# The Dice gate of a recommender kernel's attention sums: from one ScalarE and one VectorE operation to two VectorE operations

## The chip, the cores and the metric

The kernel runs on one core of one Trainium2 chip. Its time is the device time of that core in microseconds (us). In what follows PE is TensorE, DVE is VectorE, ACT is ScalarE, POOL is GpSimd and SP is SyncE, as the profile calls them.

## The reference

For 16384 users, each with 69 item ids (`batch_user`) and one label id, rows of 96 floats are taken from an embedding table of 100001 rows. An attention network gives each of the 69 rows one weight, the weighted rows are summed in 10 windows of fields, and a small network follows.

```python
def _dice(x, alpha, eps):
    p = jax.nn.sigmoid(_bn_eval(x, eps))
    return (alpha * (1.0 - p) + p) * x

u = emb[batch_user]
ql = emb[batch_label[:, 0]]
q = jnp.broadcast_to(ql[:, None, :], u.shape)
z = jnp.concatenate([q, u, q - u, q * u], axis=-1)
h = _dice(z @ W1 + b1, a1, EPS_DICE)
h = h @ W2 + b2
att = h @ W3 + b3
eff = (batch_user < ITEM_NUM)[..., None]
pre = jnp.where(eff, u * att, 0.0)
pooled = jnp.einsum('gf,bfe->bge', window, pre).reshape(u.shape[0], G * E)
x = jnp.concatenate([pooled, ql], axis=-1)
h = _dice(_bn_eval(x @ Wf1 + bf1, EPS_BN), af1, EPS_DICE)
h = _dice(_bn_eval(h @ Wf2 + bf2, EPS_BN), af2, EPS_DICE)
return h @ Wf3 + bf3
```

The change concerns the first `_dice`, on the sums `z @ W1 + b1` of 64 hidden units. With p the sigmoid of the sum x, and a the unit's alpha, it is (a + (1 - a) p) x.

## The kernel before

**Tiling.** The users are cut into 32 blocks of 512. A block has 69 chunks of 512 (user, field) places: 64 main chunks of 8 users with 64 fields each, and 5 tail chunks of one field for all 512 users. Two chunks make a pair, and the whole kernel is a sequence of 1104 pairs. All data is fp32.

**Steps.** Python unrolls everything. A dictionary `plan` holds, for each step (one pair is fetched in each), a list of work that is put out in that order on all engines; the tile framework adds the semaphores and keeps the order as written (`manual_schedule`). Each engine runs its own instructions in order. In step i, in this order, stand:

- every fourth step, `attend_rows` of the pairs i-6 to i-3: PE multiplies four y tiles by the folded second and third layer (`prow`, L414), and ACT copies the result (`row`, L416);
- `attend_tail` of pair i-3, for tail chunks alone (`pa`, L423, and DVE's `pre`, L424);
- every fourth step, `spread`: PE transposes `row` (`patt`, L431) and DVE turns it into weights for the pooling (`rw`, L436);
- `hidden` of pair i-2: PE's sums `ph` (L396 to L403), then the Dice gate that makes `y` (L405 to L407);
- ACT's own row fetches for this step (`scalar_rows`, L301, 16 rows of 384 bytes each, with the offsets loaded into registers at L286);
- `pool` of pair i-7: 16 matmuls of `rw` with the rows (`acc`) and DVE's copy into `pooled` (L470);
- `fetch` of pair i: the gathers of 128 rows each by POOL into `u` (L266), PE's transposes of them (`ptr`; the helper `read_rows` at L325 records these and the matmuls of `acc`), and for each of the two chunks DVE's copy `uT` (L376) and product `quT` (L379, or L386 in a tail chunk).

Between these, spread over the steps, stand the label rows of the next block (`q`, gathered by POOL as well, 128 gathers in all) and the final network of a finished block (`p`, L502 to L522, with gates of its own at L483 to L485, which the change leaves alone).

**Fetches.** A pair needs 8 gathers of 128 rows. Of the 8832 of all pairs, 8587 are indirect DMAs issued by POOL; the other 245 are done row by row with plain DMAs into `ring`, by SP (13952 rows) and ACT (17408 rows). A transpose or `acc` matmul that reads `ring` waits for its rows by a semaphore.

**Buffers that matter here.** `u` has 14 buffers of one pair each, and a pair is read for the last time by `pool`, 7 steps after its fetch. `ptr` has 2 PSUM buffers, `ph` has 2, `acc` has 1; `y` has 6 buffers in SBUF. `a1c` and `na1c` are columns of 128 scalars in SBUF that hold a and 1 - a.

**The gate before.** ACT makes the sigmoid from `ph` (PSUM) into `y` (SBUF), then in a second operation y becomes a + (1 - a) y in place, and DVE multiplies by `ph`.

Of the kernel before, what the change touches and what calls it, by code (L numbers as in the profile page):

```python
# [14 lines left out]
AF = mybir.ActivationFunctionType  # L15
ALU = mybir.AluOpType
# [46 lines left out]
def chunk_of(c):  # L63

    n, k = divmod(c, NCH)
    if n == NBLK - 1 and k >= EARLY:
        k = NMAIN + k - EARLY if k < EARLY + NTAIL else k - NTAIL
    return n, k
# [47 lines left out]
def rec_kernel(  # L116
# [12 lines left out]
    nc = tc.nc  # L129
# [68 lines left out]
    a1c = NEAR.of(wn, "a1")  # L198
    na1c = const.tile([P, 1], F32, name="na1c")
# [189 lines left out]
    def hidden(i, uT, quT):  # L389

        ph = ps_h.tile([P, 512], F32, tag="h", name=f"ph{i}")
        places = [chunk_of(2 * i + j) for j in range(2)]
        sums = [ph[j * H1 : (j + 1) * H1, :] for j in range(2)]
        for (n, k), p in zip(places, sums):
            if k >= NMAIN:
                nc.tensor.matmul(p, Cq, qTs[n % 2], start=True, stop=False)  # L396
        for j, ((n, k), p) in enumerate(zip(places, sums)):
            if k < NMAIN:
                nc.tensor.matmul(p, As[n % 2][:, k // 4, :], uT[j], start=True, stop=False)  # L399
            else:  # L400
                nc.tensor.matmul(p, A, uT[j][0:E], start=False, stop=False)  # L401
        for j, p in enumerate(sums):
            nc.tensor.matmul(p, Wp, quT[:, j, :], start=False, stop=True)  # L403
        y = ypool.tile([P, 512], F32, tag="y", name=f"y{i}")
        nc.scalar.activation(y, ph, AF.Sigmoid, scale=S_DICE)  # L405
        nc.scalar.activation(y, y, AF.Identity, bias=a1c, scale=na1c)  # L406
        nc.vector.tensor_mul(y, ph, y)  # L407
        return y

    def attend_rows(b, n):  # L410
# [156 lines left out]
    def hidden_of(k):  # L567
        return lambda: ys.__setitem__(k, hidden(k, *hs[k]))
# [186 lines left out]
```

## Time and profile before

| What | Value |
|---|---|
| Median of 3 runs | 13779.89 us (13749.68 to 13785.55) |
| The profiled execution's own time | 10926.71 us |
| Its span, first to last instruction | 10924.9 us |
| Granted TensorE clock in it, mean | 0.745 |
| PE busy | 8862.0 us (81%) |
| POOL busy | 8226.3 us (75%) |
| DVE busy | 4285.5 us (39%) |
| ACT busy | 1897.5 us (17%) |
| DMA engines, mean | 42 GB/s |

The profile is one execution. Its own time is 1.8 us above its span, and 2853 us below the median of the runs: the runs were longer than the profiled execution by a factor of 1.261. A duration read from the profile is therefore a part of 10926.71 us.

A line of the groups reads: line of the code, engine, operation, output<-input by the tiles' names, shapes, number; then total busy time in us and mean of one in ns; then the idle time of that engine just before these instructions, and what ended most of it. "issue" means that the engine waited for nothing that the profile shows. A line of the timeline reads: start in us, length in us, engine, line, operation, tiles, number, and in brackets the idle time before it.

### The profile page before, as it was taken

The page shows a single profiled execution, that of the slowest core. Times are in us where ns is not written, and L with a number is a line of the kernel's source. Part 1 is how long each engine was busy: PE and PEld are TensorE (multiplying, and loading weights), DVE is VectorE, ACT ScalarE, POOL GpSimd, SP SyncE. Part 2 cuts the span into 40 slices and gives each one's busy share as a digit, 9 for nine tenths or more (in the row PEclk, how much of TensorE's full clock was granted, in tenths as well). Part 3 has the DMA queues.
Part 4 walks back from the last instruction along what each step waited for, and adds up shares of the span by engine and source line. Part 5 has one row for each costly group of instructions (what it writes and reads, how often), then busy time and mean ns, then how long its engine had stood idle before and what let it go on. Part 6 is the DMA issues. An engine that isn't in the chain of part 4 may idle for free.

```text
span 10924.9 us, 172203 instructions
## 1 busy us (share of the span) xinstructions
PE 8862.0 (81%) x41797; PEld 4319.5 (40%) x41797; DVE 4285.5 (39%) x7535; ACT 1897.5 (17%) x2761; POOL 8226.3 (75%) x8721
## 2 busy tenths in 40 slices
PE   7878878788887888888878778878888887888878
PEld 3333434343333344333433333334343333433335
DVE  4334333333333333433333333333333333333334
ACT  1111111111111111111111111111111111111112
POOL 7777777777777777777777777777777777777776
PEclk7767777777777777767777777777777777777777
DMA  2212211121111212212111121112212112122111
GB/s 49 42 42 44 42 42 41 42 44 42 42 42 42 44 41 42 42 41 44 42 42 41 42 44 42 42 42 42 44 42 42 42 41 44 42 42 41 42 41 36
DMA packets 344467, 458.51 MB, mean 42 GB/s; under 512 B 202354, under 2 KB 202866, under 8 KB 343330
## 3 DMA queue, kind: packets, MB, share of 16 engines
q0 software_dynamic: 278880, 428.92, 18.7%
q1 hardware_dynamic: 29762, 11.82, 0.5%
q10 hardware_dynamic: 34816, 6.75, 0.4%
q8 instruction: 336, 5.51, 0.2%
q14 instruction: 673, 5.51, 0.2%
HBM read 446.74 MB, written 0.07 MB: 41 GB/s over the span
## 4 chain that ended last, share of the span: by engine, by line
POOL 49%; issue 21%; PE 17%; DMA 12%; DVE 0%; ACT 0%; ACTq 0%; POOLq 0%; DVEq 0%
POOL u L266 48%; DMA u<-in_rows,ids 12%; PE p L502 4%; PE acc L325 4%; PE ph L399 3%; PE ph L403 2%; PE ptr L325 2%; POOL q L266 1%; PE prow L414 1%; PE pa L423 1%; PE ph L396 0%; PE ph L401 0%; PE pc L348 0%; PE patt L431 0%; ACTq L301 0%
## 5 line engine op out<-in xcount | busy, mean ns | idle before, releaser
L266 POOL DMA_INDIRECT u<-in_rows,ids x8587 | 8104.3, 944 | 2620.1 <-issue 2428.2
L325 PE MATMUL ptr<-ident,u 128*96 128x128 f32 x8587 | 2002.8, 332 | 1940.1 <-DMA u<-in_rows,ids 1892.9
L407 DVE TENSOR_TENSOR y<-ph,y 128x512 f32<-128x512 f32 x1104 | 763.5, 692 | 4377.1 <-ACT y L406 4119.6
L325 PEld LDWEIGHTS ptr<-ident,u 128*96 128x96 f32 x8587 | 1139.7, 149 | 2701.4 <-DMA u<-in_rows,ids 2262.6
L325 PEld LDWEIGHTS acc<-rw,u 128*96 128x96 f32 x15930 | 1677.0, 187 | 1204.3 <-issue 977.6
L376 DVE COPY uT<-ptr 96x512 f32<-96x512 f32 x2208 | 1494.1, 677 | 1488.6 <-PE ptr L325 1485.2
L325 PE MATMUL acc<-rw,u 128*96 128x20 f32 x15930 | 1792.5, 258 | 57.8 <-DVE rw L436 41.7
L405 ACT ACTIVATE y<-ph 128x512 f32<-128x512 f32 x1104 | 658.6, 597 | 6308.6 <-PE ph L403 5822.7
L399 PE MATMUL ph<-uT,A 128*64 128x512 f32 x4096 | 1649.8, 883 | 0.0
L403 PE MATMUL ph<-quT,wn 96*64 96x512 f32 x4416 | 1585.2, 788 | 0.0
L379 DVE TENSOR_TENSOR quT<-ptr,qT 96x512 f32<-96x512 f32 x2048 | 1380.2, 674 | 0.0
L406 ACT ACTIVATE y<-y,wn,na1c 128x512 f32<-128x512 f32 x1104 | 898.1, 813 | 36.6
L403 PEld LDWEIGHTS ph<-quT,wn 96*64 96x64 f32 x4416 | 440.7, 188 | 1041.5 <-issue 1040.8
L502 PE MATMUL p<-pooled,wf 96*100 96x512 f32 (+1 forms) x1400 | 693.1, 644 | 0.0
L399 PEld LDWEIGHTS ph<-uT,A 128*64 128x64 f32 x4096 | 264.1, 175 | 616.2 <-issue 608.8
L416 ACT COPY row<-prow 128x512 f32<-128x512 f32 (+1 forms) x277 | 161.6, 583 | 1791.9 <-PE prow L414 1179.1
L470 DVE COPY pooled<-acc 96x160 f32<-96x160 f32 x1008 | 419.9, 417 | 117.6 <-PE acc L325 116.9
L414 PE MATMUL prow<-y,v 128*32 128x512 f32 x2208 | 453.6, 891 | 1.4 <-DVE y L407 1.1
L502 PE MATMUL p<-pre,V 96*100 96x512 f32 (+1 forms) x700 | 394.9, 710 | 3.0 <-DVE x L485 2.7
L502 PEld LDWEIGHTS p<-pooled,wf 96*100 96x100 f32 x1400 | 259.5, 198 | 332.6 <-issue 332.6
L436 DVE SCALAR_TENSOR_TENSOR rw<-patt,bb,wn 128x320 f32<-128x320 f32 x554 | 276.2, 539 | 143.6 <-PE patt L431 142.9
L431 PE MATMUL patt<-ident,row 128*128 128x128 f32 x1108 | 224.9, 340 | 25.1 <-DVE pre L424 22.7
(72 smaller groups left out, 2445.8 us busy)
## 6 DMA issues: line engine op xcount, KB each, us to landing
ring<-in_rows ACTq DMA_DIRECT2D x17408, 0.4 KB
ring<-in_rows SPq DMA_DIRECT2D x13952, 0.4 KB
u<-in_rows,ids POOLq DMA_INDIRECT x8587
ids<-in_idx SPq DMA_DIRECT2D x8, 560.0 KB, 3.9
q<-in_emb,ids POOLq DMA_INDIRECT x128
wf<-in_far SPq DMA_DIRECT2D x1, 1209.0 KB, 6.4
wn<-in_near SPq DMA_DIRECT2D x1, 236.0 KB, 2.8
ids<-in_idx SPq DMA_DIRECT2D x1, 140.0 KB, 2.3
```

The source lines that it names most:

```text
L266: nc.gpsimd.indirect_dma_start(out=dst, out_offset=None, in_=table, in_offset=bass.IndirectOffsetOnAxis(ap=index, axis=0),)
L325: ins = op(out, ring[:, at[0]].bitcast(F32) if at else u[:, 4 * (c % 2) + t, :], other, **how)
L376: nc.vector.tensor_copy(uT[j][0:E], ptr)
L379: nc.vector.tensor_tensor(quT[:, j, :].rearrange("e (s f) -> e s f", f=FM), ptr.rearrange("e (s f) -> e s f", f=FM), by_field(q[:, k * NS ...
L399: nc.tensor.matmul(p, As[n % 2][:, k // 4, :], uT[j], start=True, stop=False)
L403: nc.tensor.matmul(p, Wp, quT[:, j, :], start=False, stop=True)
L405: nc.scalar.activation(y, ph, AF.Sigmoid, scale=S_DICE)
L406: nc.scalar.activation(y, y, AF.Identity, bias=a1c, scale=na1c)
L407: nc.vector.tensor_mul(y, ph, y)
L414: nc.tensor.matmul(pr[32 * k : 32 * (k + 1), :], v2, ys[b + k], start=True, stop=True)
L470: nc.vector.tensor_copy(pooled[n][:, :, k * NS : (k + 2) * NS].rearrange("e g s -> e s g"), pa.rearrange("e j s g -> e (j s) g"),)
L502: nc.tensor.matmul(p1, w[:, h * DH : (h + 1) * DH], x, start=(k == 0), stop=(k == KTOP - 1))
```

## The change

ACT makes the sigmoid s of the sums alone. DVE then makes the gate in two operations, each with one operand in PSUM and one in SBUF: first y = (s (1 - a)) x, then y = (x a) + y, with x in `ph`. The second reads what the first wrote.

```diff
         y = ypool.tile([P, 512], F32, tag="y", name=f"y{i}")
         nc.scalar.activation(y, ph, AF.Sigmoid, scale=S_DICE)
-        nc.scalar.activation(y, y, AF.Identity, bias=a1c, scale=na1c)
-        nc.vector.tensor_mul(y, ph, y)
+        nc.vector.scalar_tensor_tensor(y, y, na1c, ph, ALU.mult, ALU.mult)
+        nc.vector.scalar_tensor_tensor(y, ph, a1c, y, ALU.mult, ALU.add)
         return y
```

Nothing else differs. The line numbers stay the same: L406 was ACT's second operation and is DVE's first one, L407 was DVE's multiplication and is DVE's second operation.

## The prediction

> **What bounds the kernel now.** I first read the page's engine rows, then the groups, because busy shares alone would point at TensorE (81%) and not at POOL (75%). The groups and the waits say otherwise. From the page:
>
> ```profile
> span 10924.9 us, 172203 instructions
> PE 8862.0 (81%) x41797; PEld 4319.5 (40%) x41797; DVE 4285.5 (39%) x7535; ACT 1897.5 (17%) x2761; POOL 8226.3 (75%) x8721
> ...
> L266 POOL DMA_INDIRECT u<-in_rows,ids x8587 | 8104.3, 944 | 2620.1 <-issue 2428.2
> L325 PE MATMUL ptr<-ident,u 128*96 128x128 f32 x8587 | 2002.8, 332 | 1940.1 <-DMA u<-in_rows,ids 1892.9
> L407 DVE TENSOR_TENSOR y<-ph,y 128x512 f32<-128x512 f32 x1104 | 763.5, 692 | 4377.1 <-ACT y L406 4119.6
> ...
> L405 ACT ACTIVATE y<-ph 128x512 f32<-128x512 f32 x1104 | 658.6, 597 | 6308.6 <-PE ph L403 5822.7
> ...
> L406 ACT ACTIVATE y<-y,wn,na1c 128x512 f32<-128x512 f32 x1104 | 898.1, 813 | 36.6
> ```
>
> POOL's idle time is "issue": it waits for nobody. With the 128 gathers of q there are 8715 gathers, each 0.944 us long and followed by 0.305 us of issue (2660.8 us of idle over 8715). 8715 x 1.249 = 10885 us of a span of 10924.9. In the timeline the last gather ends at 10887.7, so 37 us follow it, and the first starts at 3.3. POOL's wait list shows no single wait above 0.3 us apart from one of 2.0 at the start. TensorE waits 1893 us in 2264 pieces for what POOL fetches, DVE 4120 us for L406, ACT 5823 us for TensorE. TensorE's 81% is no sign of a bound: its granted clock averages 0.745[...]. The gathers' rhythm is the bound; everything else runs beside it.
>
> [...] The two new operations have one SBUF tensor, one PSUM tensor and a pointer scalar in SBUF[...]. L424 already has that kind of operands (pa in PSUM, bb a pointer, uT in SBUF), so I looked at gathers beside it in the timeline:
>
> ```profile
> 1048.57 0.94 POOL L266 DMA_INDIRECT u<-in_rows,ids  x1 [0.30 <-issue]
> ...
> 1049.82 0.94 POOL L266 DMA_INDIRECT u<-in_rows,ids  x1 [0.30 <-issue]
> ...
> 1050.10 1.40 DVE L424 SCALAR_TENSOR_TENSOR pre<-pa,bb,uT 96x512 f32<-96x512 f32 x2
> ...
> 1051.07 0.94 POOL L266 DMA_INDIRECT u<-in_rows,ids  x1 [0.30 <-issue]
> ...
> 1052.32 0.95 POOL L266 DMA_INDIRECT u<-in_rows,ids  x1 [0.31 <-issue]
> ```
>
> Two such operations lie over two gathers, and the starts stay 1.25 us apart. Over all records of the trace the mean distance from one gather's start to the next is 1249.1 ns where an L424 lies over it, 1248.7 where none does. [...] the trace has 0.692 us for L407. [...] I price the dependent pair at two full durations and a gap.
>
> **The change part by part.** *Removed:* 1104 ACT operations of 0.813 us = 898 us (L406 of before), and 1104 DVE multiplications of 0.692 = 764 us. *Added:* 2208 SCALAR_TENSOR_TENSOR on DVE, 128x512. The nearest rows are L424 (0.739 median, 96x512) and L485 (0.751, 100x512); lower bound the 0.692 of L407, upper 0.80 for a pointer read that costs more. I take 0.745: 2208 x 0.745 = 1645, so DVE gains 881 us (764 to 1003), from 4286 to 5167 us or 47% of the span. That is hidden: on POOL nothing depends on it directly. The built order shows the rows of PE, POOL and SP unchanged, ACT 1104 fewer, DVE 1104 more.
>
> *The chain of one y.* Before (timeline at 5007): sigmoid from 5006.99 to 5007.59, L406 from 5007.62 to 5008.43, DVE from 5008.46 to 5009.15: 1.56 us from the sigmoid's end. After: a hop of 0.04, 0.745, a gap of 0 to 0.2 for the second operation's wait on the first (I take 0.05), 0.745: 1.58 us (1.42 to 1.84). So y, and the PSUM bank ph, come at about the same time. Behind the waiting second operation DVE queues pooled (L470), uT (L376) and quT (L379), for which TensorE's transposes wait through two ptr banks. In 1032 of 1104 cases DVE stood idle for L406, 4.0 us on average, so it starts earlier and ends no later. In the other 72 it was behind, and pays up to 881/1104 = 0.80 us: 57 us in all, on DVE. What covers that is the 1893 us that TensorE waits for gathers, and behind it u's 14 buffers, of which a pair is released 7 pairs later: POOL would be held only when TensorE falls several pairs (of 9.9 us each) behind. Cost 0. If that cover went, the next thing late would be the transposes and then POOL's waits for u.
>
> *ACT's row fetches* (L301, 16 a pair, and the offset loads L286) stand behind L406 in ACT's queue. In the timeline they start at 5007.68, just after L406 was issued at 5007.62, so they move forward by about 0.63 us a pair. No matmul on ring waits in the trace (idle 0.0 before them), and SP's queue is not touched: gain 0, unless ACT is the bound (below).
>
> *Head and tail.* Before the first gather nothing changes. In the 37 us behind the last one, the chain runs through matmuls, the row copy and g (L483, L484), and has no L406 after 10887; allow 0.3 us either way.
>
> **Sum:** 10926.7 us (the profiled execution's own time, 1.8 around its span) + 0, give or take 1 us. The runs' median is 13779.89, 1.261 times that. The profile does not show why. [...] I take the change as 0 of the median too: **13780 us**. A measurement of this kernel can tell about 0.3% (41 us) from no change; its three runs span 0.26%.
>
> **Rivals.** *Slower: DVE and gathers exclude each other in the timed runs.* Suppose the unseen 2853 us are gathers held up by DVE: 2853 / 4286 = 0.67 us for each busy us. Then 881 more cost 587: 14367 us, 4.3% slower. It decides from 0.047 us for each added us of DVE (41 / 881). The one fact for it is the unexplained gap; against it, gathers are not longer beside any DVE operation in the trace (0.5 ns). Chance 0.10. *TensorE is the bound in the timed runs.* Were its clock 0.5 throughout, its busy time would be 8862 x 0.745 / 0.5 = 13204, close to the median. The chain of y is then still as long, so mostly no change; if the 72 late cases all count, 57 us more: 13837. Chance 0.09, of which 0.04 for over 0.3%. *Faster: ACT's queue is the bound in the timed runs.* In the trace ten row fetches take 2.95 us, so 17408 take 5135; with 544 offset loads at 2.17 and 1898 busy this is 8216 us or 75%. ACT would have to stretch 1.68 times for 13780 while the whole stretches 1.26. It would gain 1104 x 0.63 = 696: 13084. Chance 0.09. *The change does not do what it says:* excluded, the rows were counted above.
>
> **How the numbers follow.** Gathers remain the bound and nothing moves: 0.64, with TensorE's unchanged part 0.05 gives 0.69 within 0.3%. Slower: 0.10 + 0.04 + 0.04 for a small unseen cost = 0.18. Faster: 0.09 + 0.04 for a small version of ACT's relief = 0.13. The range leaves out the two large rivals (0.19) and takes in the small ones, which I let reach 1% either way: 13640 to 13920.
>
> **What would show it.** Right: L266 again 8587 times at 944 with idle only for issue; DVE near 5170 us, ACT near 1000; the new lines near 0.745; DVE's wait for ACT now for L405 and about 0.8 us shorter each. Wrong: gathers longer or further apart than 1.25 us, POOL waiting for PE's acc, or a span that changes by more than 33 us (0.3% of 10926.7). If the span stays and the timed median moves, the fault is in carrying the profiled execution over to the timed runs.

## The result, and the profile after

The changed kernel took 13663.19 us (median of 5 runs, 13658.30 to 13688.42), the kernel before 13762.13 us beside it: a ratio of 0.9932, 95% interval 0.9915 to 0.9949. That is a gain of 0.7%, where no change was forecast.

The program's runs come in two lengths: about 10.93 ms and about 13.6 to 13.8 ms. The profiled execution of before that the prediction rests on was of the **short kind**; the runs that were to be predicted, and the profile after, are of the **long kind**. In both, a gather (in the changed kernel 0.944 us in the short kind and 0.945 in the long one), the sigmoid (0.597 in both) and the two gate operations (0.747 and 0.751 against 0.745 and 0.751) themselves take the same time. What differs is the time between them: POOL's idle time before the gathers is 2620 us in the one and 5285 in the other.

The page of the changed kernel, long kind. The line that begins with "PE 28%" is the chain that ended last: the work and the waits met when one goes back from the last instruction, each time to what released it, as shares of the span. ACTq in it is ACT's sequencer, which issues ACT's row fetches and holds them in one queue with ACT's operations (in the prediction's trace each of the 1088 groups of 16 fetches stands whole between two ACT operations, and the earliest operation behind one starts 0.04 us after its end):

```profile
span 13660.8 us, 171082 instructions
PE 9255.3 (68%) x41797; PEld 4797.0 (35%) x41797; DVE 5106.9 (37%) x8639; ACT 992.1 (7%) x1657; POOL 8237.3 (60%) x8721
...
PE 28%; issue 25%; ACTq 21%; another core or an unknown queue 14%; DVE 10%; ACT 2%; POOL 1%; DMA 0%; POOLq 0%
...
L266 POOL DMA_INDIRECT u<-in_rows,ids x8587 | 8115.1, 945 | 5284.9 <-issue 2284.1
...
L406 DVE SCALAR_TENSOR_TENSOR y<-y,na1c,ph 128x512 f32<-128x512 f32 x1104 | 822.7, 745 | 4219.3 <-issue 2329.2
L325 PE MATMUL ptr<-ident,u 128*96 128x128 f32 x8587 | 1706.4, 350 | 718.5 <-issue 526.8
...
L405 ACT ACTIVATE y<-ph 128x512 f32<-128x512 f32 x1104 | 658.9, 597 | 8332.7 <-remote 3222.0
...
L407 DVE SCALAR_TENSOR_TENSOR y<-ph,wn,y 128x512 f32<-128x512 f32 x1104 | 829.1, 751 | 39.0
```

A gather still takes 0.945 us and the sigmoid 0.597, but POOL is idle for 5285 us in place of 2620, and TensorE hardly waits for gathers before `ptr`: 11 us, where the prediction's profile had 1893. The chain hardly runs through POOL: 1% in place of 49% in the short kind. The waits of POOL in the same profile say for what it waits (us in all, times, longest; "remote" is a release that the records do not show):

```profile
POOL u L266 <- remote: 1416.6, 593, 3.9
POOL u L266 <- PE ptr L325: 887.6, 189, 51.9
POOL u L266 <- PE acc L325: 228.2, 30, 20.5
```

So in the long kind TensorE is late and the gathers wait for it. Worked out from the records, a gather starts when 6.1 pairs of transposes are still to be done (median), so that `u` is full; in the short kind it is 0.4.

The same kernel in the short kind (after_again below), from its page:

```profile
span 10927.5 us, 171082 instructions
PE 8861.9 (81%) x41797; PEld 4341.1 (40%) x41797; DVE 5172.4 (47%) x8639; ACT 1001.1 (9%) x1657; POOL 8225.5 (75%) x8721
...
POOL 49%; issue 21%; PE 17%; DMA 12%; DVE 0%; ACTq 0%; ACT 0%; POOLq 0%
...
L266 POOL DMA_INDIRECT u<-in_rows,ids x8587 | 8103.9, 944 | 2619.6 <-issue 2418.3
L406 DVE SCALAR_TENSOR_TENSOR y<-y,na1c,ph 128x512 f32<-128x512 f32 x1104 | 824.4, 747 | 3370.0 <-ACT y L405 3323.3
...
L405 ACT ACTIVATE y<-ph 128x512 f32<-128x512 f32 x1104 | 658.7, 597 | 6989.2 <-PE ph L403 6618.5
L407 DVE SCALAR_TENSOR_TENSOR y<-ph,wn,y 128x512 f32<-128x512 f32 x1104 | 829.2, 751 | 39.0
```

Here the gathers run as before and the change moves nothing: 10927.50 against 10927.89 us, ratio 1.0000 (0.9991 to 1.0008).

### The profile page after: what moved, and what is told of

It reads as the page before. It is cut to its first block, busy times and chain, and to the rows that moved or that the text cites. A ratio compares the mean times of both kernels' runs of the same rounds, so it can differ in the third digit from the quotient of the medians.

```text
span 13660.8 us, 171082 instructions
## 1 busy us (share of the span) xinstructions
PE 9255.3 (68%) x41797; PEld 4797.0 (35%) x41797; DVE 5106.9 (37%) x8639; ACT 992.1 (7%) x1657; POOL 8237.3 (60%) x8721
## 4 chain that ended last, share of the span: by engine, by line
PE 28%; issue 25%; ACTq 21%; another core or an unknown queue 14%; DVE 10%; ACT 2%; POOL 1%; DMA 0%; POOLq 0%
ACTq L301 18%; PE acc L325 6%; PE ptr L325 5%; PE ph L399 4%; PE p L502 4%; PE ph L403 4%; ACTq L286 2%; DVE uT L376 2%; DVE quT L379 2%; PE prow L414 2%; DVE y L406 2%; DVE y L407 2%; ACT y L405 1%; DVE pooled L470 1%
## 5 line engine op out<-in xcount | busy, mean ns | idle before, releaser
L325 PE MATMUL acc<-rw,u 128*96 128x20 f32 x15930 | 2014.5, 272 | 1908.8 <-issue 1280.6
L325 PEld LDWEIGHTS acc<-rw,u 128*96 128x96 f32 x15930 | 1897.3, 205 | 2981.6 <-issue 2047.5
L406 DVE SCALAR_TENSOR_TENSOR y<-y,na1c,ph 128x512 f32<-128x512 f32 x1104 | 822.7, 745 | 4219.3 <-issue 2329.2
L325 PE MATMUL ptr<-ident,u 128*96 128x128 f32 x8587 | 1706.4, 350 | 718.5 <-issue 526.8
L403 PE MATMUL ph<-quT,wn 96*64 96x512 f32 x4416 | 1611.4, 720 | 202.7 <-issue 196.4
L325 PEld LDWEIGHTS ptr<-ident,u 128*96 128x96 f32 x8587 | 1284.6, 170 | 937.9 <-issue 701.2
L403 PEld LDWEIGHTS ph<-quT,wn 96*64 96x64 f32 x4416 | 447.0, 175 | 1277.5 <-issue 1275.0
L407 DVE SCALAR_TENSOR_TENSOR y<-ph,wn,y 128x512 f32<-128x512 f32 x1104 | 829.1, 751 | 39.0
L414 PE MATMUL prow<-y,v 128*32 128x512 f32 x2208 | 645.9, 840 | 249.1 <-DVE y L407 133.0
L502 PE MATMUL p<-pre,V 96*100 96x512 f32 (+1 forms) x700 | 423.9, 750 | 156.2 <-issue 107.4
L431 PE MATMUL patt<-ident,row 128*128 128x128 f32 x1108 | 257.0, 367 | 387.2 <-issue 205.8
L423 PE MATMUL pa<-y,vrep 64*96 64x512 f32 x320 | 189.8, 973 | 268.7 <-DVE pre L424 152.0
```

The source lines that it names most:

```text
L325: ins = op(out, ring[:, at[0]].bitcast(F32) if at else u[:, 4 * (c % 2) + t, :], other, **how)
L406: nc.vector.scalar_tensor_tensor(y, y, na1c, ph, ALU.mult, ALU.mult)
L407: nc.vector.scalar_tensor_tensor(y, ph, a1c, y, ALU.mult, ALU.add)
L414: nc.tensor.matmul(pr[32 * k : 32 * (k + 1), :], v2, ys[b + k], start=True, stop=True)
L502: nc.tensor.matmul(p1, w[:, h * DH : (h + 1) * DH], x, start=(k == 0), stop=(k == KTOP - 1))
```

## The experiments

The experiments come in sets. The kernels of one set ran side by side on one chip, and each ratio is against the kernel before in the same set. Which kind a set met could not be chosen; within a set it was always the same. The theories:

- **A:** in the long kind the time goes with the number of instructions recorded (172203 before, 171082 after, also 0.7% apart).
- **B:** in the long kind ACT's queue, where the next sigmoid stands behind 16 row fetches, is on the path, and L406 stood in that queue. (Its first form in the expectations made that queue the only bound.)
- **C:** every engine is slower by one factor.
- **D:** TensorE's completions come at a limited rate in the long kind and set the pace.
- **E:** the gain came on VectorE, whose 1104 separate waits for a semaphore before L407 (0.021 us each in the prediction's trace, none in the one after) fell away.

### First set: long kind

**before_again**, the kernel before.

> The kernel before, unchanged, for a second profiled execution. Its runs have a median of 13762 us, its profiled execution 10926.7. Theory A (time goes with the number of instructions that all engines issue, at 13762 us / 172203 recorded instructions = 79.9 ns each, and the profiled execution of before was of another kind): about 13760 us, with POOL, ACT and SP standing still in pieces of 0.7 to 2 us as in the trace of after. Theory B (ACT's queue is the bound of these runs, and L406 stood in it): about 13760 us too, ACT's queue full nearly all the time, the other engines standing still only where they wait for it. If it comes at 10930 with gathers 1.25 us apart, the two kinds of execution mix by chance.

Measured: 13638.94 us, beside runs of the same program with a median of 13611.84. Its trace is the long-kind partner of the profile shown ahead of the prediction:

```profile
ACTq 29%; issue 27%; PE 25%; another core or an unknown queue 8%; ACT 6%; DVE 4%; POOL 2%; DMA 0%; DVEq 0%; POOLq 0%
...
L266 POOL DMA_INDIRECT u<-in_rows,ids x8587 | 8100.5, 943 | 5280.1 <-issue 2255.6
...
L406 ACT ACTIVATE y<-y,wn,na1c 128x512 f32<-128x512 f32 x1104 | 897.5, 813 | 36.7
```

Gathers stretch in their spacing, not in their duration: a gather is 0.944 us in the short kind and 0.943 here, and POOL's idle time before them 2620 us and 5280. So theory C falls. The 16 row fetches of a pair take 5.05 us from the first to the last in the short kind and 8.66 here.

**dve_tiny4** (`pad` is a scratch tile of one element):

```diff
         nc.vector.scalar_tensor_tensor(y, ph, a1c, y, ALU.mult, ALU.add)
+        for _ in range(4):
+            nc.vector.memset(pad, 0.0)
```

> The changed kernel with four memsets of one element behind every y on VectorE: 4416 instructions of some 0.06 us more, on an engine that is 37% busy. Theory A: 4416 x 79.9 ns = 353 us more than the changed kernel's 13663, about 14016 us, 1.8% above the kernel before. Theory B: ACT's queue is untouched, so it stays near 13663 us, 0.7% below the kernel before.

Measured: 0.9967 of the kernel before (0.9951 to 0.9983); a memset took 0.059 us. Theory A's 1.8% are excluded. It is 0.35% above the 0.9932 that the changed kernel had in another set, and the intervals just miss each other (0.9951 and 0.9949), so VectorE's time may count a little.

**no_sp_rows** and **no_act_rows**:

```diff
-SP_CHUNKS = [2 * (10 * s + 8) + 1 for s in range(109)]
+SP_CHUNKS = []
```

```diff
-ACT_CHUNKS = [2 * (8 * s + 11) for s in range(136)]
+ACT_CHUNKS = []
```

> The changed kernel without SP's row fetches: 109 chunk tiles are gathered by POOL instead, and SP issues about 28300 instructions fewer. Theory A: (171082 - 28300) x 79.9 ns = 11408 us. Theory B: ACT's queue is untouched, so about 13663 us. If gathers alone bound it: 8824 x 1.249 + 40 = 11061 us.

> The changed kernel without ACT's row fetches: 136 chunk tiles are gathered by POOL instead, and ACT issues about 35400 instructions fewer. Theory A: (171082 - 35200) x 79.9 ns = 10857, below the gathers' own 8851 x 1.249 + 40 = 11095 us, so about 11100. Theory B: ACT's queue is emptied, so the gathers bound it too: about 11100 us. This run tells A and B from theory C (neither matters and every engine is slower by one factor, 1.26): 8851 x 1.249 x 1.25 + 50 = 13870 us.

Measured: 0.9912 (0.9893 to 0.9932) without SP's fetches, 0.9842 (0.9819 to 0.9866) without ACT's. Theory A falls altogether: it asked for more than 2000 us less than the changed kernel. With 0.9932 of this set's kernel before for the changed one, 13519 us (an estimate, it was not in this set), 28000 instructions fewer gave about 20 us and 35000 about 105. Without SP's fetches the kernel can hardly be told from the changed one; without ACT's it gains another 0.9%. ACT's queue is on the path, but it is not the only bound: the gathers' 11095 us are far away.

### Second and third set: short kind

**after_again**, the changed kernel, with **act_pad** (`pad` is a scratch tile of 128x32, set to 0 once):

```diff
         nc.scalar.activation(y, ph, AF.Sigmoid, scale=S_DICE)
+        for _ in range(2):
+            nc.scalar.activation(pad, pad, AF.Identity, bias=a1c, scale=na1c)
         nc.vector.scalar_tensor_tensor(y, y, na1c, ph, ALU.mult, ALU.mult)
```

**act_ident**:

```diff
         nc.scalar.activation(y, ph, AF.Sigmoid, scale=S_DICE)
+        nc.scalar.activation(y, y, AF.Identity)
         nc.vector.scalar_tensor_tensor(y, y, na1c, ph, ALU.mult, ALU.mult)
```

and **half_acc**, in `pool`:

```diff
-            for t in range(4):
+            for t in range(0, 4, 2):
...
-                    pa[:, j, 2 * t : 2 * t + 2, :].rearrange("e n g -> e (n g)"),
+                    pa[:, j, 2 * t : 2 * t + 4, :].rearrange("e n g -> e (n g)"),
...
-                    rw[:, t, j, :],
+                    rw[:, t : t + 2, j, :],
```

> The changed kernel once more, to be compared with the next two on the same chip: 0.993 of the kernel before, as first measured. Theory B (a core slowed everywhere by late completions, in which ACT's queue of row fetches stands before the sigmoid, and L406 stood in that queue) and its rivals expect the same here.

> The changed kernel with two small ACT operations (128x32, on a scratch tile that nobody else reads, the second waits for the first) between the sigmoid and the row fetches. They hold ACT's queue for about 0.8 us a pair, as L406 held it for 0.63, and leave the chain of y (sigmoid, then DVE's two operations) as it is. Theory B: the gain is lost, 0.997 to 1.002 of the kernel before, and the sigmoid starts about 0.6 us later after its sums than in after_again. Theory E (the gain came on VectorE, from 1104 waits for semaphores that L407 no longer makes): 0.993, as after_again.

> The changed kernel with an identity of ACT on y between the sigmoid and VectorE's first operation, so L406 of before stands in ACT's queue again and y comes 0.84 us later. Theory B: the queue costs what it cost before (the 0.7% are lost) and y's delay costs more: 1.002 to 1.010 of the kernel before. Theory E: VectorE keeps its gain and only y's delay costs: 0.995 to 1.000.

> Leaves out half of the weighted sums: 4 matmuls of 40 columns a pair in place of 8 of 20, each with the rows of one gather, so the rows of the other gathers are not summed. TensorE has 32000 of 86000 instructions fewer by half, that is about 16300 matmul and weight-load records fewer, and all other engines are unchanged. Theory D (TensorE's completions come at a limited rate in these executions, some 0.13 us per instruction, and set the pace): 16300 x 0.13 = 2100 us less than the changed kernel, 0.84 of the kernel before. If only TensorE's busy time counts: 2048 x 4 x 2 x 0.085 = at most 700 us less when all of it lies on the path, 0.945. If TensorE's number of instructions does not matter: 0.99.

This set met the short kind, for which none of these gave a number. Measured: 1.0000, 1.0001, 1.0004 and 0.9999, each with an interval of at most 0.1% to either side. A queue that is 0.9 us fuller, a y that is 0.66 us later, a fifth less of TensorE's instructions: nothing moves while the gathers are the bound. The third set met the short kind as well (act_pad2 and half_acc2 repeat the two kernels; with them went **no_rows** and **no_rows_before**, the changed kernel and the kernel before with both lists of chunks empty and `NSB = 2`).

> The kernel of act_pad again: the changed kernel with two small ACT operations between the sigmoid and the row fetches, about 0.8 us a pair in ACT's queue. There are two kinds of executions: one of about 10927 us, in which gathers follow each other every 1.25 us, and one of about 13600 us, in which every engine stands still at times. In the first kind every theory expects 1.000 of the kernel before, as act_pad showed. In the second kind, theory B (L406 stood in ACT's queue of row fetches, before the next sigmoid) expects 0.997 to 1.002 of the kernel before, theory E (VectorE's 1104 waits that fell away) 0.993.

> The kernel of half_acc again: half of the weighted sums are left out, 16300 matmul and weight-load records of TensorE fewer. In the executions of about 10927 us: 1.000 of the kernel before. In those of about 13600: theory D (TensorE's completions come at a limited rate there and set the pace) 0.84 to 0.90, a theory in which TensorE's instructions do not matter 0.99.

> The changed kernel with no row fetches at all: 8960 gathers. In the executions of about 10927 us the gathers bound it: 8960 x 1.249 + 40 = 11231 us, 1.028 of the kernel before. In those of about 13600: theory B, ACT's and SP's parts of the gain together, 0.97 to 0.98 of the kernel before, and with the next kernel the same within 0.2%, since nothing stands behind L406 any more; theory E, 0.7% less than the next kernel.

> The kernel before (its gate with L406 on ACT) with no row fetches at all, the partner of no_rows: 11231 us in the executions of about 10927. In those of about 13600: theory B, the same as no_rows within 0.2%, 0.97 to 0.98 of the kernel before; theory E, 0.7% above no_rows.

Measured: 1.0001, 0.9997, and 11232.05 and 11232.61 us. The last two were expected at 11231 from the number of gathers alone. That is the bound of the short kind, and the change does nothing beside it.

### Fourth set: long kind

**act_pad3** and **half_acc3**, the same two kernels.

> The changed kernel with two small ACT operations between the sigmoid and the row fetches, about 0.8 us a pair in ACT's queue, on another chip. Where the kernel before takes about 10930 us: 1.000 of it. Where it takes about 13600 us: theory B (L406 stood in ACT's queue of row fetches, before the next sigmoid) 0.997 to 1.002, theory E (VectorE's 1104 semaphore waits that fell away) 0.993.

> Half of the weighted sums left out, 16300 matmul and weight-load records of TensorE fewer, on another chip. Where the kernel before takes about 10930 us: 1.000 of it. Where it takes about 13600 us: theory D (TensorE's completions come at a limited rate there and set the pace) 0.84 to 0.90; if TensorE's instructions do not matter, 0.99.

Measured: act_pad3 1.0048 (1.0031 to 1.0064), half_acc3 1.0027 (1.0019 to 1.0036). The first decides between B and E: with the queue filled again the gain is gone, though VectorE's part of the change is untouched. It even goes past what was expected, as the two operations hold the queue longer than L406 did. From the start of a sigmoid to the first row fetch behind it, where no offset load stands between, it takes a median of 0.07 us in the changed kernel, 0.70 with L406 (before_again) and 1.00 here. Theory D falls: a fifth of TensorE's instructions less, and it takes longer, not shorter. Why longer stays open; the records show only that the 16 row fetches of a pair took 9.8 us there and that ACTq had 34% of the chain.

The chain that ended last in act_pad3's profile, to be read against 21% for ACTq in the changed kernel:

```profile
ACTq 30%; issue 27%; PE 20%; another core or an unknown queue 8%; DVE 7%; ACT 6%; POOL 2%; DMA 0%; POOLq 0%
...
L409 ACT ACTIVATE pad<-pad,wn,na1c 128x32 f32<-128x32 f32 x2208 | 901.9, 408 | 37.0
```

### Fifth set: long kind

**no_act_before** (the kernel before with `ACT_CHUNKS = []`) and **after_again2** (the changed kernel).

> The kernel before, with L406 on ACT, but without ACT's row fetches (136 chunk tiles gathered by POOL instead): the partner of no_act_rows, which took 0.984 of the kernel before where that takes about 13600 us. There, theory B (L406 delays the row fetches and with them the next sigmoid) expects no difference to no_act_rows, 0.982 to 0.987, since no row fetch stands behind L406 any more; theory E (VectorE's part of the change made the gain) expects 0.7% more, 0.991. Where the kernel before takes about 10930 us, the gathers bound it: 8851 x 1.249 + 40 = 11095 us, 1.015.

> The changed kernel on the same chip: 0.993 of the kernel before where that takes about 13600 us, 1.000 where it takes about 10930.

Measured: after_again2 0.9923 (0.9904 to 0.9941), the gain once more. no_act_before 0.9815 (0.9795 to 0.9836), against 0.9842 (0.9819 to 0.9866) for no_act_rows in the first set: with no row fetch behind L406, taking it off ACT gains nothing. (It may lose 0.3%; the intervals overlap.) Together with act_pad3 this leaves theory B: **the gain is the room in ACT's queue ahead of the row fetches.** The chains of no_act_before and no_act_rows (second line) show the queue gone, and TensorE and releases that the records do not name in its place:

```profile
PE 44%; another core or an unknown queue 26%; issue 17%; DVE 6%; POOL 5%; ACT 3%; DMA 1%; DVEq 0%; POOLq 0%
...
PE 42%; another core or an unknown queue 24%; issue 19%; DVE 9%; POOL 4%; ACT 1%; DMA 1%; POOLq 0%; ACTq 0%
```

### Last set: short kind

**act_ident2** repeats act_ident; **lag8** has `POOL_LAG = 8`, with pair c-16 added to the pooling list of the last steps.

> The changed kernel with an identity of ACT on y between the sigmoid and VectorE's first operation: ACT's queue holds what it held before, and y comes 0.66 us later. Where the kernel before takes about 10930 us: 1.000 again. Where it takes about 13600: theory B, the gain is lost and y's delay costs a little, 1.000 to 1.008; theory E, 0.993 to 1.000.

> The changed kernel with the pooling one pair later (POOL_LAG 8 in place of 7), so that TensorE has one pair's time more between VectorE's rw and the matmuls that read it; u's 14 buffers then let the gathers run 6 pairs ahead in place of 7. Where the kernel before takes about 10930 us: 1.000, gathers bound it. Where it takes about 13600: if TensorE's waits for rw (274 us of 13661 in the changed kernel) lie on the path, 0.975 to 0.985; if the pace is set elsewhere, 0.992 as the changed kernel.

Measured: 1.0004 and 0.9999. This met the short kind, so both questions for the long kind, how much y's delay costs there and whether the wait for rw does, stay open.

### The queue in numbers

From the records, means in us. "Rows" is from the first to the last of the 16 fetches of a pair; "wait" from the recorded end of a pair's last `ph` matmul (L403) to the start of its sigmoid; "ACTq" is its share of the chain that ended last.

| Kernel, kind | Rows | Wait | ACTq |
|---|---|---|---|
| before, short | 5.05 | 0.35 | 0% |
| after_again, short | 5.05 | 0.24 | 0% |
| before_again, long | 8.66 | 6.82 | 29% |
| after, long | 8.71 | 6.21 | 21% |
| act_pad3, long | 8.73 | 7.14 | 30% |
| no_act_before, long | none | 4.89 | 0% |
| no_act_rows, long | none | 4.85 | 0% |

The wait follows the time for which the queue is held, though these kernels ran in different sets. Without L406 the row fetches start 0.62 us earlier, and the wait is 0.61 shorter; with the two operations of act_pad3 they start 0.30 us later than with L406, and the wait is 0.32 longer. Where no row fetches follow, L406 makes 0.04 us of difference. Of the 1040 sigmoids of before_again that wait over 0.5 us, 741 start within 0.35 us of the end of what stands before them in ACT's queue.

Another way for L406 to cost time would be that the rows reach TensorE later. The records exclude it: the last row of a chunk is issued at least 14.9 us before TensorE's transpose reads it (before_again and the changed kernel), and TensorE stood idle for 6.4 and 5.2 us in all before these 245 transposes.

In the timeline of the changed kernel this looks as follows, first the short kind (after_again), then the long kind:

```profile
5005.81 0.60 ACT L405 ACTIVATE y<-ph 128x512 f32<-128x512 f32 x1 [1.56 <-PE ph L403]
5005.88 4.95 ACTq L301 DMA_DIRECT2D ring<-in_rows  x16
5006.45 0.75 DVE L406 SCALAR_TENSOR_TENSOR y<-y,na1c,ph 128x512 f32<-128x512 f32 x1 [3.55 <-ACT y L405]
5007.23 0.75 DVE L407 SCALAR_TENSOR_TENSOR y<-ph,wn,y 128x512 f32<-128x512 f32 x1
```

```profile
5020.40 0.60 ACT L405 ACTIVATE y<-ph 128x512 f32<-128x512 f32 x1 [6.51 <-issue]
5021.03 0.75 DVE L406 SCALAR_TENSOR_TENSOR y<-y,na1c,ph 128x512 f32<-128x512 f32 x1 [2.94 <-issue]
5021.06 9.80 ACTq L301 DMA_DIRECT2D ring<-in_rows  x16
5021.81 0.75 DVE L407 SCALAR_TENSOR_TENSOR y<-ph,wn,y 128x512 f32<-128x512 f32 x1
...
5031.14 0.59 ACT L416 COPY row<-prow 128x512 f32<-128x512 f32 x1 [10.14 <-issue]
```

The gate is the same in both. In the long kind the 16 row fetches last 9.80 us, and ACT's next operation starts 0.28 us after their end: it stood behind them. A step is 12.3 us in the long kind, of which 8.7 go to row fetches and 1.0 on average to offset loads (2.0 us in every second step).

Which version is best depends on the kind: without ACT's row fetches 0.982 to 0.984 where the kernel takes 13.6 to 13.8 ms, but 1.028 without any row fetches where it takes 10.93. (Without ACT's alone the gathers there would give about 1.015, an estimate from 8851 gathers of 1.249 us; it was not run there.) No version that was run beats both kernels on both.

## Why the prediction was wrong, step by step

- **Right, for the profiled kind:** gathers bound it (no_rows to within 0.01%), and the sum of the change is 0 (1.0000). VectorE was expected at 5167 us and measured 5172, an operation at 0.745 and measured 0.747 and 0.751, with 0.035 between the two, ACT near 1000 and measured 1001. No gather moved beside the new operations: from one start to the next it is 1.249 us with and without them.
- **Right:** the chain of y. From the sigmoid's start to the end of y it was 2.168 us before and 2.165 after (medians), in both kinds; the prediction's 0.597 + 1.58 is 2.18.
- **The step that failed:** "I take the change as 0 of the median too". The text saw the gap of 1.261 and carried the short kind's bound and covers across it; that was the author's assumption, which no trace showed. The term of ACT's row fetches, 0.63 us a pair, was put at 0 with them; it was worth 99 us, 0.09 us a pair. The runs show no common stretch: gather and sigmoid last as long in the long kind (0.945 and 0.597 us) as in the short one (0.944 and 0.597). What grows is the spacing: from one gather's start to the next it is 1.249 us in the prediction's trace and 1.556 in the one after (means).
- **The cover that was gone:** the prediction hid VectorE's and ACT's times under TensorE's wait for gathers. In the long kind that wait is all but gone (1893 us before, 22 in before_again), `u` is full, and POOL waits for TensorE. "Gain 0, unless ACT is the bound" named the right term, but the condition was too strict: ACT's queue need not be the bound, it is enough that it is part of the path (29% of the chain in before_again, 21% in the changed kernel).
- **The rival that came nearest:** "ACT's queue is the bound in the timed runs" asked for a stretch of 1.68. The row fetches show 8.66 / 5.05 = 1.71. But the queue is not full even so: 8.66 us for 1088 pairs and 544 offset loads of 2.01 make about 10500 of before_again's 13637 us. (The sum that led to 1.68 also counted L406 and the fetches issued during it one after the other.) And it priced the gain at the full 0.63 us a pair, 696 us. The wait before the sigmoid did shrink by 0.61 us (6.82 to 6.21), while the time shrank by 0.09 us a pair, a seventh. That fits a queue that is only a part of the path: taken away with all its fetches, it gives 1.6 to 1.9%. What takes up the other six sevenths was not measured.
- **Foreseen, with little weight:** "a small version of ACT's relief", chance 0.04, is what came. The range of 13640 to 13920 us took it in; that the result lies inside it is owed to this allowance and not to the forecast.
- **A reading that was off, without weight here:** of the 72 gates at which VectorE was held to be behind, the waits listed for L407 show it idle in 60 too (29, 25 and 6 pieces that end with something other than L406). The 57 us were an upper limit.
- **The rivals that fell:** gathers held up by VectorE (in the trace of the changed kernel, long kind, a gather takes 0.945 us beside the new operations and away from them), and TensorE as bound by a clock of 0.5 (the granted clock is 0.723, with TensorE busy for 68%). In the trace of before a matmul of `prow` (L414) takes a median of 0.593 us where the granted clock is 1.0 and 1.061 where it is 0.5, so the rival's scaling by the clock was sound to about a tenth.

## What to carry to other kernels

Compare the profiled execution's time with the median of the runs before anything else. Here they differed by a factor of 1.261, and the profile showed another regime: the cover found in it ("TensorE waits for gathers anyway", 1893 us) was down to 22 us in before_again. L406, 0.81 us on a queue that also issues DMAs, cost what stood behind it: taking it off gained 0.7% with the row fetches there and nothing without them (0.9842 with it off ACT, 0.9815 with it on). So read who comes next in such a queue, the next sigmoid here, and not the busy share of the engine, which was 14% for ACT in before_again.

## What the runs showed of the hardware that was not expected

One and the same program takes 10.93 ms in some sets of runs and 13.6 to 13.8 in others, while its gathers and its operations on ACT and VectorE last as long (0.944 us and 0.945 for a gather of the changed kernel, 0.597 and 0.597 for its sigmoid, 0.747 and 0.745 for its L406). The chip's number does not tell the two apart: number 10 stands in the record of the first set (long) and of the last (short). In the long kind ACT's register moves ahead of the row fetches take 100 ns on average in place of 29 (after and the prediction's trace), a tenth of them over 600; and where VectorE is already idle, the copy of `acc` starts a median of 1.0 us (before_again) and 3.0 us (after) past the recorded end of its matmul, in place of 0.038. The long kind's trace also holds fewer semaphore updates (58590 in after, 221112 in after_again), so that what it names as the end of a wait is less sure. What makes an execution long was not tried, and stays open; so does what sets the pace in the long kind beside ACT's queue.
